# One step earlier in the input and one product form changed: image 1's load in layer 0, v's projection of images 6 and 7 in layer 1

## The chip, the cores and the metric

The kernel runs on one core of one Trainium2 chip. The metric is the device time of one execution in microseconds; 2955.44 us is the median of five executions before the change (2954.72 to 2956.1). Names of engines: PE is TensorE (matmuls), PEld its weight loads, DVE is VectorE, ACT is ScalarE, POOL is GpSimd, SP is the engine whose queue issues nearly all DMAs. All data are float32.

## What is computed

Eight images of 384 channels and 32 x 32 points pass through two attention layers. Cut to what matters here:

```python
# layer 0 (8 heads of 48): x = x + proj(softmax(q k^T * 48**-0.5 + relative_bias) v), qkv from group_norm(x)
# layer 1 (6 heads of 64): t = tokens of x
t = t + attn(layer_norm(t))     # q, k normalised per head, softmax, v, output projection
t = t + ffn(layer_norm(t))      # sign weights, groups of images 0..4 only; images 5..7 get zero
# v = layer_norm(t) @ qkv_w[v].T : for each image 1024 tokens x 384 channels -> 384
```

## The kernel before

**Units.** Both layers work image by image, and an image's attention is a list of units `(pair, h, m2)`: a pair of heads, one half of the queries, a quarter of the keys (32 units per image in layer 0, 24 in layer 1). `scores` makes two 128 x 1024 tiles of scores in PSUM (L746 in layer 0, L1722 in layer 1), DVE adds the relative bias in layer 0 (L757, two instructions per unit), ACT takes the exponent, and `weigh` of the unit two before multiplies with v (L777, L1771). PSUM has four such tiles for everything (`mm2`), SBUF nine tiles of 128 x 1024 for layer 0 (`etile`) and sixteen for layer 1 (`wtile`).

**Order.** The order of the instructions on each engine and queue is the order in which the program issues them. Side work is hung on a list, `later`: `later.after(n, work)` issues `work` at the n-th following step, and there is one step after each unit (`later.step()`), so a number there is a place in the order and not a time. An engine and the SP queue wait at each entry for what it needs, and everything issued after it on the same engine waits too.

**Layer 0, image 0.** While image 0's 32 units run, side work is done once for the whole kernel. The relative bias `grow` is loaded from a table in DRAM (`grow_load`, four DMAs of 114 KB into `oT`, L486) and turned round by ACT or DVE in turn (`grow_turn`, L496 and L498), one part per unit up to unit 16. The q and k weights are cut in two parts and a mixed part (`_cut_weights`, DVE, units 9 to 15 and 20 to 27) and stored to `cut`; v's weights are cut in the same way by `cut_weights_v` (L606 on: mask, subtract, mix, scale, three stores of 192 KB for each of three chunks) to `cut_v`, beginning at units 16, 17 and 18, the second halves two units later. Image 1's input `xn` is loaded at unit 12 (`load`, three DMAs of 512 KB, L343), and its group norm follows: `measure` (two statistics instructions per chunk, L513) at units 16, 17 and 18, a gather of two small DMAs, `scatter` (L527 on DVE, four POOL instructions, two DMAs) at unit 21, `apply` on ACT at units 24, 25 and 26. The masks for image 1's cut input follow at units 28, 29 and 31.

**One-pass products.** From image 1 on, layer 0 makes its projections as three products of cut operands: a high part (a mask clears the lowest 12 bits), a low part and a mixed part, each of type float32r. The profile has one matmul instruction and one weight load for each of these products, and two of each for a plain float32 matmul. `Ahead.project_v` (L698) makes layer 0's v so: 72 matmuls per image. Its stationary operand is `parts[..][:, ts(2 * m2 + i, P)]`, 128 neighbouring columns.

**Layer 1.** Images 0 to 4 have a feed-forward part, images 5 to 7 none. For images 6 and 7 `attention_inputs` makes q and k as one-pass products (`project_cut`, six blocks in the order 0, 1, 2, 4, 3, 5) from `Parts`, which holds the cut image, with weights that `_Cut.load` (L161, 576 KB each) brings into four slots (three in a tile `wc`, one in `more_cut`, shown as `wx`). Blocks 2 and 3 stay in their slots for good; blocks 0 and 1 are loaded at unit 3 of the image before, blocks 4 and 5 into the same slots when blocks 0 and 1 are done. Then `project_v` makes v as plain float32: 24 matmuls (48 instructions) per image, L1659. Its stationary operand takes every eighth column:

```python
xt[:, k].rearrange("c (p m) -> c m p", m=MT)[:, 2 * m2 + i],
wv[:, k], start=(k == 0), stop=(k == KC - 1),
```

DVE evicts it with a multiplication by the tokens' inverse deviation (L1669).

Of the kernel before, what the change touches and what calls it, by code (L numbers as in the profile page):

```python
# [19 lines left out]
F32 = mybir.dt.float32  # L20
F32R = mybir.dt.float32r
# [6 lines left out]
P = 128  # L28
# [27 lines left out]
NG = 5  # L56
# [43 lines left out]


BLOCKS = [(pair, s) for pair in range(KC) for s in range(2)]
BLOCKS1 = [(0, 1), (0, 0), (1, 1), (2, 1), (1, 0), (2, 0)]


# [94 lines left out]
class _Weights:  # L200
# [50 lines left out]
    def load_part(self, k, w):  # L251
        at = k * 3 * C
        self.nc.sync.dma_start(w, self.ready[:, at : at + 2 * C])

    def cut(self, k, w, tile):
        return _cut_weights(self.nc, k, w, tile, self.there)

# [14 lines left out]
        self.nc.sync.dma_start(self.image, self.x1[0].rearrange("(k p) n -> p k n", p=P))  # L272


def _layer0(tc, ins, x1, sums, shared, weights, beside):

# [6 lines left out]
    with ExitStack() as ctx:  # L285
# [306 lines left out]
                    )  # L592
            return qk

        BB = len(BLOCKS) // 2
        cut = dram.tile([len(BLOCKS), P, 3, KC, P], F32, tag="cut", name="cut", bufs=1)
        cut_v = dram.tile([P, 3, KC, C], F32, tag="cutv", name="cutv", bufs=1)

        def cut_tile(name):
            return etile(name)[:, 0 : 2 * C]  # L600

        def cut_weights_v(k):

            w = wv[:, k]
            t = etile(f"cv{k}")
            high, mixed = t[:, 0:C], t[:, HALF : HALF + C]  # L606

            def first():
                _masked(nc, high, w)
                nc.sync.dma_start(cut_v[:, 0, k], high)  # L610
                nc.vector.tensor_sub(w, w, high)

            def second():
                _mixed(nc, mixed, w, high)
                nc.sync.dma_start(cut_v[:, 2, k], mixed)
                nc.vector.tensor_scalar_mul(w, w, CUT)
                nc.sync.dma_start(cut_v[:, 1, k], w)

            first()
            later.after(2, second)  # L620

        class Ahead:

# [290 lines left out]
        for k in range(KC):  # L914
# [7 lines left out]
            )  # L922
            for at, stage in zip(((9, 11, 13, 15), (20, 21, 22, 23), (24, 25, 26, 27))[k], stages):
                later.after(at + 1, stage)
        for k in range(KC):
            later.after(17 + k, lambda k=k: cut_weights_v(k))
        for b in range(B):
            held = []
            for i, u in enumerate(units):
                done = held.pop(0) if len(held) == LAG else None  # L930
                held.append(
                    (u, scores(b, qk, u, lambda: weigh(b, *done) if done else None))
                )
                if i == (12 if b == 0 else 1) and b + 1 < B:
                    xn = load(b + 1)
                    for at, stage in zip(
                        (5, 6, 7, 10, 13, *((14, 15) if b == 0 else (13, 13))),
                        group_norm(b + 1, xn),
                    ):
                        later.after(at, stage)  # L940
                if i == 3 and b > 0:
                    project_out(b - 1, residuals(b - 1, etile), range(NF0))
                if b == B - 1:
                    for at, work in beside:
                        if at == i:
                            work()
                later.step()
                if i == 28 and b == 0:
                    cuts = _Cut(
                        nc, cut, BLOCKS,  # L950
                        shared.pool.tile([P, KC * 3 * C], F32R, tag="w", name="wc"),
                    )
                    for n in range(BB):
                        cuts.load(n)
                if b in (1, 2, 3) and i == 12:
                    t = cut_tile(f"cw{b}")
                    weights.load_part(b - 1, t)
                    for at, stage in enumerate(
                        weights.cut(
                            b - 1, t, lambda name, b=b, t=t: t if name == "cl" else cut_tile(f"{name}1{b}")  # L960
                        )
                    ):
                        later.after(4 + at, stage)
                masks, rounds = ((28, 29, 31), ()) if b == 0 else ((25, 26, 27), (28, 29, 30))
                if b + 1 < B:
                    if i == masks[0]:
                        ahead = Ahead(b + 1, xn)
                    if i in masks:
                        ahead.mask(masks.index(i))
                    if i in rounds:  # L970
                        ahead.round(rounds.index(i))
# [373 lines left out]
            )  # L1345


def _layer1(tc, ins, x1, out, shared, start, there, before=None, check=None):

# [1 line left out]
    with ExitStack() as ctx:  # L1353
# [300 lines left out]
        def project_v(b, xt, m2, c=None, copy=nc.vector.tensor_copy):  # L1654
# [9 lines left out]
            if c is None:  # L1664
                copy(v[:, 2 * m2 : 2 * m2 + 2], pv[:, :, 0:C])
            else:
                for i in range(2):
                    m = 2 * m2 + i
                    nc.vector.tensor_scalar_mul(v[:, m], pv[:, i, 0:C], c[:, 1, m : m + 1])  # L1669
            later.step()  # L1670

        def scale_v(c, m2):
# [382 lines left out]
        def attention_inputs(b, xt, rest=(), sums=None, parts=None):  # L2055
# [17 lines left out]
            for i, n in enumerate(range(len(BLOCKS)) if parts is None else (0, 1, 2, 4, 3, 5)):  # L2073
                if parts is None:
                    project_qk(b, *BLOCKS[n], xt, qk, sq)
                else:
                    project_cut(b, n, parts, qk, sq)
                    if i < 2:
                        cuts.load(n + 4)
                    if i == 0:  # L2080
                        rest_of_units()
                if i == 1:
                    token_stats(f"a{b}", tk)
                pair = i // 2
                if i % 2 == 0 and pair > 0:
                    head(pair - 1, *((5, 4) if pair > 1 else (3, 3) if parts is None else (2, 4)))
            if parts is None:
                rest_of_units()
            for m2 in range(MT // 2):
                project_v(b, xt, m2, tk)  # L2090
            head(NP1 - 1, 4, 4)
            return qk, kc

# [17 lines left out]
        later.after(26, store_w2)  # L2111
        later.after(1, rest_of_pools)
        qk, kc = attention_inputs(0, xt)
        behind = cuts = parts = None
        for b in range(B):


# [7 lines left out]
            for i, u in enumerate(units):  # L2125
# [7 lines left out]
                if i == 3:  # L2133
# [9 lines left out]
                    if more and b > 0:  # L2143
                        if cuts is None:
# [4 lines left out]
                            )  # L2149
                            cuts.load(2)  # L2150
                            cuts.load(3)
                        cuts.load(0)
                        cuts.load(1)
                        parts = Parts(b + 1, ahead)
                        for k, at in enumerate((8, 10, 12)):
                            later.after(at - i, lambda k=k, parts=parts: parts.cut_high(k))
# [140 lines left out]
def tile_conv_attn_hybrid(ctx: ExitStack, tc: tile.TileContext, ins, out):  # L2297
    dram = ctx.enter_context(tc.tile_pool(name="x1", bufs=1, space=DRAM))
    x1 = dram.tile([B, C, N], F32, tag="x1", name="x1")
    ready = dram.tile([P, KC * 3 * C], F32, tag="ready", name="ready")  # L2300
    there = dram.tile([len(BLOCKS), P, 3, KC, P], F32, tag="there", name="there1")
    state = ctx.enter_context(tc.tile_pool(name="state", bufs=1))
    flag = state.tile([P, 1], mybir.dt.int32, tag="flag", name="flag")
    sums = state.tile([P, B, NP0, 2 * N // P], F32, tag="sums", name="sums")
    with ExitStack() as main, tc.manual_schedule():
        shared = _Shared(tc, main)
        start = _Start(tc, ready, x1, shared)
        before = _layer0(
            tc, ins, x1, sums, shared, _Weights(tc, ins, ready, there, shared),
            [(5, start.load_weights), (6, start.load_image)],  # L2310
        )
        _layer1(
            tc, ins, x1, out, shared, start, there, before,
            lambda temp: _range_check(tc, sums, flag, lambda name: temp(name, (P, HALF))),
        )

# [1 line left out]
    with tc.If(out_of_range > 0):  # L2318
        _layer0_shifted(tc, ins, x1)
        with ExitStack() as again, tc.manual_schedule():  # L2320
# [1 line left out]
            start = _Start(tc, ready, x1, shared)  # L2322
            start.load_weights()
            start.load_image()
            _layer1(tc, ins, x1, out, shared, start, there)


# [42 lines left out]
```

## Time and profile before

| what | value |
|---|---|
| median of five executions | 2955.44 us |
| the profiled execution | 2955.57 us, of which 2953.7 us span |
| PE busy | 2920.0 us, 99% of the span |
| DVE, ACT, POOL busy | 67%, 51%, 17% |
| granted TensorE clock, mean | 0.998 |
| layer 0, image 0: from the first scores to the next image's projections | 75.41 to 202.04 us |
| layer 1, v of image 6 (L1659) | from 2660.33 to 2675.91 us |

The page's first part gives busy time, share of the span and instructions of each engine. In the timeline a row is: start in us, duration in us, engine, line, operation, output from input, shape, number of instructions, and in brackets the idle time before it and what ended it. In the table of stretches each engine has its busy time and its count, then the granted clock (1.00 is full speed), the share of the DMA engines, and GB/s.

### The profile page before, as it was taken

To read this page: it belongs to the slowest core of one execution; us is meant where nothing else is said; L and a number is where in the kernel's file an instruction comes from. 1 tells how busy PE (TensorE), PEld (TensorE's weight loads), DVE (VectorE), ACT (ScalarE), POOL (GpSimd) and SP (SyncE) were. 2 spreads that over 40 slices of the span, in tenths; PEclk is the share of its full clock that TensorE was granted. 3 is DMA by queue.
4 is the path that set the end of the run, shared out by engine and by line. 5 is a ranking of instruction groups with operands and counts; after the bars stand their busy time and mean duration, and the time that the engine had idled before them with its cause. 6 is when DMAs were issued, how large, how long until landed. Compare 5 with 4: busy or idle time off the path is not lost.

```text
span 2953.7 us, 47525 instructions
## 1 busy us (share of the span) xinstructions
PE 2920.0 (99%) x19538; PEld 1692.7 (57%) x19538; DVE 1970.3 (67%) x2005; ACT 1507.9 (51%) x1846; POOL 492.7 (17%) x312
## 2 busy tenths in 40 slices
PE   8999999999999999999999999999999999999998
PEld 3345565657565666644545647647647647655553
DVE  3786858676676757564655875875875875875756
ACT  2553626354453626353553555555555555564644
POOL 3020202121110202112202202302302302301020
PEclk9999999999999999999999999999999999999999
DMA  7643141312212140323311212112112112112111
GB/s 195 177 136 94 45 128 39 114 59 70 75 52 93 25 127 17 95 80 104 80 56 31 83 32 72 67 31 72 67 32 71 67 32 72 67 40 83 40 46 39
DMA packets 131971, 214.36 MB, mean 73 GB/s; under 512 B 62144, under 2 KB 81072, under 8 KB 130368
## 3 DMA queue, kind: packets, MB, share of 16 engines
q1 hardware_dynamic: 128480, 209.39, 24.0%
q8 instruction: 157, 2.57, 0.4%
q10 hardware_dynamic: 3264, 1.82, 0.2%
q14 instruction: 70, 0.57, 0.1%
HBM read 161.83 MB, written 40.28 MB: 68 GB/s over the span
## 4 chain that ended last, share of the span: by engine, by line
PE 92%; DVE 3%; DMA 2%; ACT 1%; issue 1%; SPq 0%; POOL 0%; DVEq 0%; ACTq 0%
PE s L746 15%; PE o L777 15%; PE s L1722 11%; PE o L1771 11%; PE pg L170 6%; PE y2p L2016 6%; PE y1p L1965 5%; PE pp L845 4%; PE pv L1659 4%; PE pm L170 3%; PE pp L1868 3%; PE vg L698 2%; PE pq L1511 2%; PE pq L572 1%; PE vm L698 1%; DVE qk L1592 1%
## 5 line engine op out<-in xcount | busy, mean ns | idle before, releaser
L761 ACT ACTIVATE e<-e 128x1024 f32<-128x1024 f32 x512 | 535.2, 1058 | 345.0 <-DVE e L757 328.7
L757 DVE TENSOR_TENSOR e<-s,grow 128x1024 f32<-128x1024 f32 x512 | 601.3, 1219 | 161.9 <-PE s L746 142.5
L746 PE MATMUL s<-qk 48*64 48x512 f32 x4096 | 613.6, 592 | 6.8 <-DVE e L757 6.8
L777 PE MATMUL o<-e,v 64*64 64x512 f32 x4096 | 608.4, 590 | 1.2 <-DVE e L757 1.2
L1733 ACT ACTIVATE e<-s,kc 128x512 f32<-128x512 f32 x768 | 464.6, 695 | 173.5 <-PE s L1722 164.0
L1722 PE MATMUL s<-qk,qk 64*64 64x512 f32 x3072 | 419.0, 592 | 2.8 <-DVE oT L1781 2.6
L1771 PE MATMUL o<-e,v 64*64 64x512 f32 x3072 | 414.5, 590 | 0.0
L746 PEld LDWEIGHTS s<-qk 48*64 48x64 f32 x4096 | 229.6, 132 | 247.7 <-issue 102.4
L777 PEld LDWEIGHTS o<-e,v 64*64 64x64 f32 x4096 | 250.1, 133 | 196.0 <-issue 104.8
L1722 PEld LDWEIGHTS s<-qk,qk 64*64 64x64 f32 x3072 | 153.5, 132 | 193.7 <-issue 109.0
L1748 DVE TENSOR_TENSOR t<-t,e 128x1024 f32<-128x1024 f32 x192 | 231.1, 1222 | 45.5 <-ACT e L1733 45.4
L1771 PEld LDWEIGHTS o<-e,v 64*64 64x64 f32 x3072 | 159.3, 133 | 169.5 <-issue 142.4
L806 POOL TENSOR_TENSOR inv<-sums,over 128x16 f32<-128x16 f32 x32 | 96.0, 2999 | 853.4 <-DMA sums<-sd 787.0
L1952 DVE TENSOR_REDUCE parts<-y 128x1 f32<-128x1024 f32 x75 | 89.7, 1217 | 103.3 <-ACT y L1949 102.9
L1745 DVE TENSOR_TENSOR t<-e,e 128x1024 f32<-128x1024 f32 x96 | 114.2, 1224 | 58.4 <-ACT e L1733 58.4
L1628 POOL TENSOR_TENSOR hc<-hc,rsqrt 128x32 f32<-128x32 f32 x24 | 137.6, 5735 | 2.0
L1659 PE MATMUL pv<-wv,bx 128*128 128x384 f32 x384 | 128.3, 491 | 0.0
L1868 PE MATMUL pp<-oT,L_attn_proj_wT 128*128 128x512 f32 x288 | 126.3, 595 | 1.6 <-DVE oT L1834 1.6
L845 PE MATMUL pp<-oT,wp 128*128 128x512 f32 x288 | 125.7, 595 | 0.0
L1659 PEld LDWEIGHTS pv<-wv,bx 128*128 128x128 f32 x384 | 119.4, 314 | 9.8 <-ACT e L1733 4.1
L673 DVE SCALAR_TENSOR_TENSOR qk<-pg,qk 128x1024 f32<-128x1024 f32 x42 | 51.5, 1225 | 100.0 <-PE pg L170 73.9
L1965 PE MATMUL y1p<-lun,w 128*128 128x512 f32 x360 | 113.4, 396 | 2.7 <-DVE lun L1915 2.7
(225 smaller groups left out, 3584.7 us busy)
## 6 DMA issues: line engine op xcount, KB each, us to landing
rb<-rd SPq DMA_DIRECT2D x110, 256.0 KB
wc<-there SPq DMA_DIRECT2D x25, 576.0 KB
wc<-cut SPq DMA_DIRECT2D x24, 576.0 KB
xn<-in_x_dram SPq DMA_DIRECT2D x24, 512.0 KB
res<-in_x_dram SPq DMA_DIRECT2D x24, 512.0 KB
x<-res SPq DMA_DIRECT2D x24, 512.0 KB
bx<-x SPq DMA_DIRECT2D x8, 1536.0 KB
rq<-hi SPq DMA_DIRECT2D x48, 256.0 KB
```

The source lines that it names most:

```text
L170: self.nc.tensor.matmul(out[:, h], w[:, i, k], part[k][:, ts(h, HALF)], start=(k == 0 and i != 1), stop=(k == KC - 1 and i != 0),)
L746: nc.tensor.matmul(s[j][ts(c, QP), i], qk[pair][rows, 1, ts(4 * m2 + 2 * i + c, QP)], qk[pair][rows, 0, ts(h, HALF)], start=True, stop=True,)
L757: nc.vector.tensor_add(e.rearrange("p (i q) -> p i q", i=2), s[j], bass.AP(near.tensor, near.offset, [near.ap[0], [-QROWS * IW, 2], [1, HA ...
L761: nc.scalar.activation(e, e, AF.Exp)
L777: nc.tensor.matmul(po[ts(j, S0), r], v[keys, 2 * m2 + i, 2 * pair + j, :], es[j][keys, ts(i, HALF)], start=(m2 == 0 and i == 0), stop=(m2 ...
L845: nc.tensor.matmul(pps[b, m][:, h], (wp[:, k] if k < NF0 else wl)[:, ts(m, P)], oT[:, k, ts(h, HALF)], start=(k == 0), stop=(k == (NF0 if ...
L1659: nc.tensor.matmul(pv[:, i, 0:C], xt[:, k].rearrange("c (p m) -> c m p", m=MT)[:, 2 * m2 + i], wv[:, k], start=(k == 0), stop=(k == KC - 1),)
L1722: nc.tensor.matmul(s[j][ts(c, QP), i], qk[pair, 1][rows, ts(4 * m2 + 2 * i + c, QP)], qk[pair, 0][rows, ts(h, HALF)], start=True, stop=True,)
L1733: nc.scalar.activation(e[:, ts(i, HALF)], s[j][:, i], AF.Exp, scale=kc[:, pair, j, m : m + 1])
L1748: nc.vector.tensor_add(total[j], total[j], e)
L1771: nc.tensor.matmul(po[ts(j, D1), r], v[keys, 2 * m2 + i, at : at + D1], es[j][keys, ts(i, HALF)], start=(m2 == 0 and i == 0), stop=(m2 == ...
L1965: nc.tensor.matmul(py[m][:, h], w1[:, k, ts(m, P)], un[k][i][:, ts(h, HALF)], start=(k == 0 and i == 0), stop=(k == KC - 1 and i == 1),)
```

## The change

In layer 0, image 0, the load of image 1 moves from unit 12 to unit 16, and the steps of its group norm move closer together: `measure` at units 18, 19 and 20, `scatter` at 22, `apply` at 24, 25 and 26 as before. `cut_weights_v` returns its two halves; they are issued at units 16 and 17, 18 and 20, 21 and 28 for the three chunks.

In layer 0, images 4 to 6, layer 1's weights of v are loaded a chunk at a time at unit 12 (192 KB), cut on DVE at units 16 and 18, and stored to a new DRAM tensor `there_v` (three stores of 192 KB).

In layer 1, at unit 3 of image 5, `load_weights_v` loads the three parts of v's weights (576, 576, 384 and 192 KB): the high part into the place of `wv`, the low part into `more_cut`, the mixed part into two of the sixteen `wtile`s, which stay taken to the end of image 7's projection. So the slots for blocks of q's and k's weights become three: block 2 is loaded again for image 7, and blocks 3, 4 and 5 are loaded after blocks 0, 1 and 2. `project_v_cut` replaces `project_v` for images 6 and 7: 72 one-pass matmuls instead of 48 instructions, two PSUM tiles instead of one per step, and an eviction by ACT and DVE for each m, with factors `cs` made by two POOL instructions.

```diff
-        def cut_weights_v(k):
-            w = wv[:, k]
-            t = etile(f"cv{k}")
-            high, mixed = t[:, 0:C], t[:, HALF : HALF + C]
+        def cut_weights_v(name, w, there, k):
+            tiles = []
             def first():
+                tiles.append(etile(name))
+                high = tiles[0][:, 0:C]
                 _masked(nc, high, w)
-                nc.sync.dma_start(cut_v[:, 0, k], high)
+                nc.sync.dma_start(there[:, 0, k], high)
                 nc.vector.tensor_sub(w, w, high)
             def second():
...
-            first()
-            later.after(2, second)
+            return first, second
...
-        for k in range(KC):
-            later.after(17 + k, lambda k=k: cut_weights_v(k))
+        for k, at in enumerate(((16, 17), (18, 20), (21, 28))):
+            for when, stage in zip(at, cut_weights_v(f"cv{k}", wv[:, k], cut_v, k)):
+                later.after(when + 1, stage)
...
-                if i == (12 if b == 0 else 1) and b + 1 < B:
+                if i == (16 if b == 0 else 1) and b + 1 < B:
                     xn = load(b + 1)
                     for at, stage in zip(
-                        (5, 6, 7, 10, 13, *((14, 15) if b == 0 else (13, 13))),
+                        (3, 4, 5, 7, 9, 10, 11) if b == 0 else (5, 6, 7, 10, 13, 13, 13),
                         group_norm(b + 1, xn),
...
+                if b in (4, 5, 6) and i == 12:
+                    t = cut_tile(f"cwv{b}")[:, 0:C]
+                    weights.load_part_v(b - 4, t)
+                    for at, stage in enumerate(cut_weights_v(f"cwx{b}", t, there_v, b - 4)):
+                        later.after(4 + 2 * at, stage)
...
+        def load_weights_v():
+            high = const.tile([P, KC, C], F32R, tag="wv", name="wvh")
+            low = more_cut.rearrange("p (k c) -> p k c", k=KC)
+            nc.sync.dma_start(high.bitcast(F32), there_v[:, 0])
+            nc.sync.dma_start(low.bitcast(F32), there_v[:, 1])
+            mixed = []
+            for at, n in ((0, 2), (2, 1)):
+                t = wtile(f"wvd{at}", (P, n, C), F32R)
+                nc.sync.dma_start(t.bitcast(F32), there_v[:, 2, at : at + n])
+                mixed.extend(t[:, k] for k in range(n))
+            return [high[:, k] for k in range(KC)], [low[:, k] for k in range(KC)], mixed
+
+        def project_v_cut(b, parts, m2, cs):
+            ps = [mm2(f"v{g}{b}_{m2}") for g in "gm"]
+            for i in range(2):
+                for part in (2, 0, 1):
+                    for k in range(KC):
+                        of = (parts.high, parts.low, parts.mixed)[part][k]
+                        nc.tensor.matmul(
+                            ps[part // 2][:, i, 0:C],
+                            of.rearrange("c (p m) -> c m p", m=MT)[:, 2 * m2 + i],
+                            weights_v[part][k],
+                            start=(k == 0 and part != 1), stop=(k == KC - 1 and part != 0),
+                        )
+            for i in range(2):
+                m = 2 * m2 + i
+                nc.scalar.activation(
+                    v[:, m], ps[1][:, i, 0:C], AF.Identity, scale=cs[:, 1, m : m + 1]
+                )
+                nc.vector.scalar_tensor_tensor(
+                    v[:, m], ps[0][:, i, 0:C], cs[:, 0, m : m + 1], v[:, m], ALU.mult, ALU.add
+                )
+            later.step()
...
-                    if i < 2:
-                        cuts.load(n + 4)
+                    if i < 3:
+                        cuts.load(n + 3)
...
+                    if parts is not None:
+                        cs = small.tile([P, 2, MT], F32, tag="cs", name=f"cs{b}")
+                        for n, by in enumerate((1.0 + 1.0 / CUT, -1.0 / CUT)):
+                            nc.gpsimd.tensor_scalar(
+                                cs[:, n], tk[:, 1], by, 1.0, ALU.mult, ALU.mult
+                            )
...
+                        if b == NG:
+                            cuts.slots = cuts.slots[: BB]
+                            weights_v = load_weights_v()
                         cuts.load(0)
                         cuts.load(1)
+                        if b > NG:
+                            cuts.load(2)
```

## The prediction

> **What bounds the kernel now.** The page's first part says who is busy: PE, nearly all the time. A gain must therefore shorten PE's own work or close one of its few gaps.
>
> ```profile
> PE 2920.0 (99%) x19538; PEld 1692.7 (57%) x19538; DVE 1970.3 (67%) x2005; ACT 1507.9 (51%) x1846; POOL 492.7 (17%) x312
> ```
>
> The waits of PE come next: the largest during attention is for DVE's bias addition, and the timelines of PE, DVE and SP put it into image 0, at unit 16.
>
> ```profile
> PE s L746 <- DVE e L757: 6.8, 4, 4.0
> ...
> 133.37 2.83 PE L746 MATMUL s<-qk 48*64 48x512 f32 x11 [4.00 <-DVE e L757]
> ...
> 131.53 0.65 DVE L498 COPY grow<-oT 128x480 f32<-128x480 f32 x1 [4.75 <-DMA oT<-table]
> ...
> 119.52 1.89 SPq L818 DMA_DIRECT2D rb<-rd  x2
> 121.84 1.32 SPq L343 DMA_DIRECT2D xn<-in_x_dram  x3
> 123.26 6.70 SPq L486 DMA_DIRECT2D oT<-table  x8
> ```
>
> DVE stands 4.75 us before a turn of the bias table, whose load was issued right behind image 1's three input DMAs. A table by stretches of image 0 shows what follows: the stalled unit, then a stretch in which DVE is busy 28.44 of 30.94 us.
>
> ```profile
> 75.41:128.35 52.94, 52.94 (x478) 22.33 (x481) 44.02 (x45) 36.31 (x40) 5.50 (x3) 1.00 0.69 200
> 128.35:138.56 10.21, 6.21 (x39) 1.69 (x35) 4.85 (x6) 2.75 (x4) 0.00 (x0) 0.70 0.78 202
> 138.56:169.50 30.94, 26.94 (x231) 8.80 (x227) 28.44 (x39) 15.55 (x16) 6.27 (x6) 0.99 0.29 90
> ```
>
> For layer 1, I compare the two forms of v: the stretches of image 6's plain v and of layer 0's one-pass v, and the instructions of their lines (minimum/median/maximum ns).
>
> ```profile
> 2660.33:2675.91 15.58, 15.58 (x49) 14.75 (x48) 6.92 (x9) 1.43 (x2) 5.63 (x2) 1.00 0.16 38
> 214.91:227.40 12.49, 12.49 (x73) 12.49 (x72) 8.20 (x14) 0.00 (x0) 2.40 (x1) 1.00 0.72 203
> ...
> L1659 PEld LDWEIGHTS pv<-wv,bx x384: 312/313/338, 1420.4 to 2824.5; 128*128 128x128 f32 x192
> L1659 PE MATMUL pv<-wv,bx x384: 486/486/720, 1420.8 to 2824.9; 128*128 128x384 f32 x192
> ...
> L698 PEld LDWEIGHTS vm<-wx,xd x168: 187/188/188, 214.7 to 1221.8; 128*128 128x128 f32 x168
> L698 PE MATMUL vm<-wx,xd x168: 334/334/342, 214.9 to 1222.0; 128*128 128x384 f32 x168
> ```
>
> The one-pass form of layer 0 takes 12.49 us for 72 matmuls, 173 ns each, against 15.5 for the plain one (48 at 323 ns). But layer 0 loads neighbouring columns (188 ns a load); layer 1 takes every eighth column, and its loads last 313 ns. Under 323 ns of streaming that is hidden; under 173 it would not be. How much of a load counts is read where PE comes out of other work: the first load and matmul of a stage.
>
> ```profile
> 2660.10 0.88 PEld L1659 LDWEIGHTS pv<-wv,bx 128*128 128x128 f32 x3
> ...
> 2660.33 0.82 PE L1659 MATMUL pv<-wv,bx 128*128 128x384 f32 x2
> ...
> 1965.74 1.36 PE L1659 MATMUL pv<-wv,bx 128*128 128x384 f32 x3
> ```
>
> **The sum's base.** The profiled execution took 2955.57 us, 2953.7 of it span; it lies 0.13 above the median of 2955.44. The sum is made against 2955.57 and then lowered by 0.13.
>
> **Image 0, the load at unit 16: -6.8 us.** Units follow each other every 3.44 us; unit 16 took 10.21, so 6.77 were lost: 4.00 idle, the rest at a granted clock of 0.70 over that stretch. The three input DMAs are 1536 KB; at the 290 GB/s of the stretch 126 to 133 us they take 5.4 us, and 1.3 us of SP's issue time. Without them the table's part has only `rb` (512 KB) ahead of it and comes some 6 us earlier, more than the 4.75 that DVE waited. At unit 16 the input is behind the last table load (132.21) and the store of the q weights (134.94) and ahead of v's stores and the sums of pair 1, whose user is POOL, with no PE work waiting. It then has two units (6.9 us) to land before its statistics, for 5.4 us of bytes of which the first third suffices. Bounds: -4 (another transfer still late) to -7.
>
> **Image 0, DVE's work spread: -1.6 us.** A unit leaves DVE 3.44 - 2.36 = 1.08 us beside its two additions. By the timeline's durations (turn 0.65, statistics of a chunk 1.28, first half of v's cut 0.91, second half 0.91, q/k cut 0.55 or 0.95, aggregate 0.78, oT's addition 0.69) the extras of units 16 to 22 were 2.84, 2.88, 3.10, 0.91, 1.46, 2.42, 0.95: 14.6 us against an allowance of 7.6, so 7.0 too much; PE lost 30.94 - 7 x 3.44 = 6.9 there, of which one wait of 1.78 before the addition at 162.33 has no releaser named and falls where v's tiles wait for their stores in the queue. After: 1.56, 1.60, 2.19, 1.28, 2.74, 2.55, 1.73, together 13.65: only 0.9 less, since just one half moves out (to unit 28). The gain lies between 0.6 (0.9, less 0.3 at units 28 and 29, where 1.6 and 1.38 meet 1.08) and 2.4 (the 1.78 too); I take the middle. So DVE stays late by some 5 us here.
>
> **Closer steps of the group norm: 0.** The gather has two units instead of three: from its first DMA (151.31) to its second (153.82) and as long again is 5 us, under 6.9. From `scatter` to `apply` on ACT: aggregate at 164.93, last DMA issued 168.67, landing some 2 us on: 5.8 us under 6.9. With that cover gone ACT waits, and its exponents behind it: up to 1 us.
>
> **Layer 0, images 4 to 6: +0.4.** 1.8 us of DVE over two units, each 0.91 under the allowance of 1.08, and four DMAs of 192 KB. Nearest row: images 1 to 3 cut q and k's weights (3.0 us of DVE) and are 166.1 us apart at the start of their projections, the later ones 165.85; so 0.25 for 3.0, and 0.15 here. Bounds 0 to 0.75.
>
> **Layer 1, the loads at unit 3 of image 5: 0.** 1728 KB on SP behind image 6's input (issued 2559.2) and ahead of blocks 0 and 1; these are used at 2627.9, 60 us later. SP's next entry is at 2605.
>
> **v in one pass: +2.15 us an image, +4.3.** Old: 48 x 0.323 = 15.5. New: 72 matmuls, each behind a load of every eighth column. The bounds of their spacing: 173 ns if the load hides as in layer 0, 313 ns if a whole load lies between two matmuls. The rows above decide between them. At 1965.74 the load had no cover: three matmuls took 1.36 instead of 2 x 0.323 + 0.486 = 1.13, and the longest one 720 instead of 486: 0.23 us exposed. At 2660.10 the load began with a one-pass matmul; the next matmul came 0.23 us later, and it and its successor took 0.82 instead of 0.81. So 0.23 to 0.25 from load to streaming, and a load starts with the matmul before: spacing 0.245, 72 x 0.245 = 17.65. Cover of the rest: eviction adds eight ACT instructions per image (nearest: oT's copy, 0.59 us each, 4.7 us in all) where ACT is busy 1.43 of 15.6 us, DVE's stay eight (0.56 for 0.61); PSUM's two tiles per step are read during the next step's 4.4 us. The two POOL instructions (0.3 each) fall where POOL idles before 2653.
>
> [...]
>
> **Three weight slots: +0.2.** Block 4 is now loaded behind block 1, not block 0: its place in SP's queue is that at 2645.45 (behind `rb`), the packets there end at 2650.24, and block 4's matmuls begin at 2650.53. Block 5 waits for block 2's matmuls (2650.9) and is used at 2656.0; such a load issued at 2632.38 ended at 2636.86. Each covers by 0.3 to 0.7 us; all of PE is queued behind. Behind block 5's DMA on SP stands pair 0's chain of norms (`hd`, `hc`, `hi`, `rq`), some 3 us later now; its user on DVE is issued after v's third step, at about 2673.5, and `rq` would land by 2669. Bounds 0 to 2.
>
> **Two tiles fewer of sixteen in layer 1: +0.4.** Units 13 to 17 hold six exponents, two totals, four folded sums and two or three of the next image's: 14 or 15. So for a few units an exponent waits for `weigh` of the unit before the last, about 0.5 us, on ACT, which has 1 us per unit spare. Bounds 0 to 5 (0.5 us in five units of two images).
>
> **Sum.** -6.8 - 1.6 + 0.4 + 4.3 + 0.2 + 0.4 = -3.1: 2952.5 from the profiled execution, 2952.4 against the median. That is 0.1%, less than the 0.2% (5.9 us) that a measurement of this kernel can tell from no change.
>
> **The rivals.**
> - Loads hide: spacing 0.173, v 12.5, -3.0 an image instead of +2.15. Sum -3.1 - 10.3 = -13.4: 2942. For it, layer 0's stage; against it, the 0.23 us between load and matmul in three places. 9%.
> - Slower: a whole load of 313 ns between matmuls: 22.5 us, +7 an image, sum -3.1 - 4.3 + 14 = +6.6: 2962. Beyond a spacing of 0.267 us ((15.5 + 3.7)/72) the kernel is slower than before, beyond 0.307 by 0.2%. For it, the loads' own durations; against it, matmuls that start before a load's record ends. 10%.
> - Image 0's stall doesn't go: a later part of the table, the statistics or `apply` takes its place, and 2 of 8.4 us are won: 2959. For it, SP's queue is in order and DVE is overfull to unit 22; against it, the bytes above. 9%.
> - Fourteen tiles bind for eight units an image, 0.5 to 1 us each: +8 to +16, 2960 to 2968. 6%.
> - The likeliest, as summed, 66%, its own range 2949.5 to 2956.
>
> **Range and chances.** 2947 to 2960.5 leaves out the first rival, most of the second and part of the fourth: about 2 in 10. Faster by over 0.2% (under 2949.5): the first rival and a tenth of the likeliest, 16%. Slower by over 0.2% (over 2961.4): two thirds of the second, half of the fourth, a little of the rest, 12%. Within: 72%.
>
> **What would show it.** Right: no wait of DVE for `oT<-table` near 131 us and full clock there; DVE still nearly full in units 17 to 23 with PE losing 4 to 6 us; v of images 6 and 7 17 to 18 us long with PEld busy throughout. Wrong: v at 12.5 or 22 us, a wait of a load at block 4, or waits before exponents in units 13 to 17 of images 5 and 6.

## The result: slightly slower, and the profile after

The changed kernel takes 2957.97 us (median of 24 executions) against 2955.39 us (44 executions of the kernel before, on the same chips): a ratio of 1.001, with a 95% interval of 1.0004 to 1.0015. The forecast of 2952.4 us had the wrong sign. The change is small, but effects of 4 to 16 us lie in it with different signs; that 2957.97 still lies within the stated range of 2947 to 2960.5 is luck, because terms that the sum did not have stand against each other. The profiled execution took 2962.07 us, of which 2960.3 us span; it lies 4.1 us above its median, while that of before (2955.57 us) lies 0.2 above its own. So the stages are compared between the two profiles, and the totals between medians.

The page's first part for the changed kernel gives the busy time of each engine:

```profile
PE 2920.6 (99%) x19586; PEld 1700.4 (57%) x19586; DVE 1976.6 (67%) x2017; ACT 1516.1 (51%) x1862; POOL 488.8 (17%) x316
```

PE's busy time is the same as before to 0.6 us. The answer is therefore not in the sums, but in the gaps. PE's waits after:

```profile
PE pm L171 <- DMA wc<-there: 11.7, 3, 5.6
PE ph L450 <- DMA w<-in_L_conv_mlp_w_dram: 8.0, 2, 7.6
PE s L750 <- DVE e L761: 3.9, 4, 1.5
PE pp L1913 <- DVE oT L1879: 3.7, 4, 1.4
```

The wait for DVE in layer 0's attention has gone from 6.8 to 3.9 us. At the top stands a wait that the table of before did not have: the projections of q and k in layer 1 (`pm`, L171) wait for a load of weights (`wc`). The table of stretches gives the stages that the prediction spoke of (us; busy time and count of PE, PEld, DVE, ACT, POOL; granted clock, DMA share, GB/s): image 0 up to unit 16, unit 16 and what follows it, then a block of image 6's projection and image 6's v.

```profile
75.37:128.32 52.95, 52.95 (x478) 22.29 (x481) 45.24 (x47) 36.30 (x40) 5.51 (x3) 1.00 0.65 185
128.32:138.63 10.31, 10.31 (x100) 3.90 (x96) 9.63 (x14) 7.08 (x8) 0.00 (x0) 1.00 0.91 290
138.63:169.50 30.87, 28.43 (x256) 10.32 (x252) 29.64 (x37) 18.35 (x20) 6.57 (x6) 1.00 0.39 111
2639.74:2646.14 6.40, 6.40 (x18) 5.08 (x19) 0.00 (x0) 1.02 (x1) 4.79 (x2) 0.63 0.03 8
2655.73:2673.14 17.41, 17.41 (x74) 17.23 (x73) 6.91 (x9) 5.68 (x10) 5.63 (x2) 1.00 0.14 33
```

In the second row, 10.31 us hold 100 matmuls at full clock, where they held 39 before: three units instead of one. In the last row v takes 17.41 us for its 72 one-pass matmuls, with PEld busy throughout. The fourth row is block 4 of image 6's q and k: 18 records in 6.40 us at a granted clock of 0.63.

Set side by side, the start of each stage on PE (first matmul, before and after) tells where the time goes. Negative is earlier after the change:

| stage | before, us | after, us | difference | change since the row above |
|---|---|---|---|---|
| projections after layer 0's image 0 | 201.97 | 194.55 | -7.42 | -7.42 |
| attention of image 5, layer 1 | 2542.32 | 2530.37 | -11.95 | -4.53 |
| q and k of image 6 | 2627.88 | 2615.65 | -12.23 | -0.28 |
| v of image 6 | 2660.33 | 2655.73 | -4.60 | +7.63 |
| attention of image 6 | 2676.91 | 2674.13 | -2.78 | +1.82 |
| q and k of image 7 | 2777.26 | 2775.24 | -2.02 | +0.76 |
| v of image 7 | 2809.70 | 2815.77 | +6.07 | +8.09 |
| attention of image 7 | 2826.28 | 2834.17 | +7.89 | +1.82 |

So: 7.4 us won in image 0; 4.5 us won after it, in images whose code the diff barely touches; 15.7 us lost before v, in the projections of q and k; 3.6 us lost in v itself.

The loss before v is one wait per image. PE's timeline at block 4 of image 6, and its first row in image 7:

```profile
2639.74 2.04 PE L171 MATMUL pm<-pw,wc 128*128 128x512 f32 x4 [5.44 <-DMA wc<-there]
2641.59 1.05 PE L171 MATMUL pm<-xd,wc 128*128 128x512 f32 x2
2642.44 3.86 PE L171 MATMUL pg<-pw,wc 128*128 128x512 f32 x12
2646.14 1.09 PE L171 MATMUL pm<-pw,wc 128*128 128x512 f32 x4
...
2799.46 2.04 PE L171 MATMUL pm<-pw,wc 128*128 128x512 f32 x4 [5.57 <-DMA wc<-there]
```

SP's queue just ahead of it:

```profile
2632.03 1.15 SPq L1870 DMA_DIRECT2D rb<-rd  x2
2633.22 1.05 SPq L162 DMA_DIRECT2D wc<-there  x2
```

PE was ready for block 4 at 2639.74 - 5.44 = 2634.30, only 1.1 us after the load had been issued behind `rb`. With it went block 5's load (x2): from 2633.22 to 2639.74 the DMA engines moved 259 GB/s, 1.69 MB, nearly what `rb` (512 KB) and both transfers of 576 KB hold together, and block 4's weights came 6.5 us after their issue. Then the gap costs a second time. The granted clock after it, from the table of stretches:

```profile
2639.74:2642.44 2.70, 2.70 (x6) 2.12 (x7) 0.00 (x0) 0.00 (x0) 1.09 (x2) 0.50 0.07 18
2642.44:2644.00 1.56, 1.56 (x5) 1.27 (x4) 0.00 (x0) 1.02 (x1) 1.56 (x1) 0.50 0.00 0
2644.00:2646.14 2.14, 2.14 (x9) 1.69 (x9) 0.00 (x0) 0.00 (x0) 2.14 (x1) 0.90 0.00 0
2646.14:2648.00 1.86, 1.86 (x9) 1.50 (x8) 1.23 (x1) 0.33 (x1) 0.86 (x1) 1.00 0.05 8
```

The clock is 0.50 for more than 4.2 us; block 4 takes 6.40 us, where the same block before took 4.30 (2646.46 to 2650.76). The wait and the slow block, 5.44 + 2.10, make 7.5 of the 7.63 us.

Theory after this reading: block 4's late load cost some 15.7 us in two images, the distance of v's columns some 5 us each, and without both the changed kernel would beat the one before. Rivals: the loss belongs to the changed order of work in general (three slots, fourteen tiles) and would not go with the load; v's matmuls are slow for another reason than their columns; and the 4.5 us in the middle are noise between two executions, or come from something that the change does unnoticed.

### The profile page after: what moved, and what is told of

Its sections match the earlier page's. It is cut to its first block, busy times and chain, and to the rows that moved or that the text cites. A ratio compares the mean times of both kernels' runs of the same rounds, so it can differ in the third digit from the quotient of the medians.

```text
span 2960.3 us, 47672 instructions
## 1 busy us (share of the span) xinstructions
PE 2920.6 (99%) x19586; PEld 1700.4 (57%) x19586; DVE 1976.6 (67%) x2017; ACT 1516.1 (51%) x1862; POOL 488.8 (17%) x316
## 3 DMA queue, kind: packets, MB, share of 16 engines
q10 hardware_dynamic: 3264, 1.82, 0.2%
## 4 chain that ended last, share of the span: by engine, by line
PE 90%; DVE 4%; DMA 2%; ACT 2%; issue 1%; SPq 0%; POOL 0%; DVEq 0%; ACTq 0%
PE s L750 15%; PE o L781 14%; PE s L1767 11%; PE o L1816 10%; PE pg L171 6%; PE y2p L2061 6%; PE y1p L2010 5%; PE pp L849 4%; PE pm L171 3%; PE pv L1669 3%; PE pp L1913 3%; PE vg L702 2%; PE pq L1521 2%; PE pq L577 1%; DMA rb<-rd 1%
## 5 line engine op out<-in xcount | busy, mean ns | idle before, releaser
L1602 DVE SCALAR_TENSOR_TENSOR qk<-pg,qsq 128x1024 f32<-128x1024 f32 x36 | 57.7, 1603 | 97.0 <-PE pg L171 68.3
L2010 PE MATMUL y1p<-un,w 128*128 128x512 f32 x360 | 112.7, 394 | 0.3 <-ACT qsq L1537 0.3
```

The costliest lines, as they stand in the source:

```text
L2010: nc.tensor.matmul(py[m][:, h], w1[:, k, ts(m, P)], un[k][i][:, ts(h, HALF)], start=(k == 0 and i == 0), stop=(k == KC - 1 and i == 1),)
```

## The experiments

Each result is the median of 4 to 11 executions (given as n) beside the kernel before on the same chip. That kernel's median varied between 2957.1 and 2959.3 us there, so ratios are compared, or starts of stages; each kernel has one profiled execution.

**The two halves alone.** `img0` is the kernel before with the edits in layer 0's image 0; `v_only` is the changed kernel without them.

```diff
 # v_only, against the changed kernel
-                if i == (16 if b == 0 else 1) and b + 1 < B:
+                if i == (12 if b == 0 else 1) and b + 1 < B:
...
-        for k, at in enumerate(((16, 17), (18, 20), (21, 28))):
-            for when, stage in zip(at, cut_weights_v(f"cv{k}", wv[:, k], cut_v, k)):
-                later.after(when + 1, stage)
+        for k in range(KC):
+            later.after(17 + k, lambda k=k: cut_v_as_before(k))
```

> The edit of image 0 alone (input at unit 16, v's cut spread), layer 1 as before. Theory A (image 0 gives about 7.4 us, and the changed kernel loses them in layer 1 at block 4's weights): 2948 us, the projections after image 0 begin at 194.6 instead of 202.0 us. Theory B (image 0's gain is given back later in layer 0 or in the feed-forward images): 2953 to 2956. One-pass matmuls of 512 columns in the feed-forward part (y1p, y2p) stay 0.232 us apart if their pace of 0.227 in the changed kernel has to do with the edit of layer 1; 0.227 if it has to do with image 0's edit.

> The edit of layer 1 alone (with the cuts in layer 0's images 4 to 6), image 0 as before. Theory A: slower by some 10 us (2965): block 4's wait of 5.5 us plus 2 us of slowed clock in each of two images, v 17.4 us instead of 15.6 in each, less some 4 us if the feed-forward matmuls go at 0.227. Theory C (block 4's wait is an accident of the shifted times): the wait of the matmuls for the block's load is absent or under 1 us and the time is 2958 to 2960.

Measured: `img0` 2949.04 us (n = 6), ratio 0.9968 (0.9956 to 0.9981); `v_only` 2969.14 us (n = 5), ratio 1.0035 (1.0022 to 1.0049), both against 2957.44. Image 0's edits gain 8.4 us, layer 1's lose 11.7; together that is +3.3, where the changed kernel measured +2.6. In `img0` the projections after image 0 start at 194.87 us, 7.1 earlier than before. In `v_only`'s trace image 0 alone was 3.0 us slower than in that of before, with the same code there: its waits for DVE were 7.8 and 2.6 us. From the first scores to the next image's projections, the five traces with image 0 as before (`before`, `v_only`, `pad`, `pad64`, `pad256`) take 126.6 to 129.5 us, the six with both edits 119.0 to 119.2. The trace of before is the shortest of its five, which can explain why the medians give image 0 more than the 7.1 to 7.4 us of the traces.

**Block 4's load one step earlier.** In the changed kernel `project_cut` ends with a step of `later`, and that step issues the pair's `rd` and `rb` on SP ahead of the load. `early` issues the load first, for blocks 3, 4 and 5 alike, and changes nothing else.

```diff
-                    project_cut(b, n, parts, qk, sq)
+                    project_cut(b, n, parts, qk, sq, step=False)()
                     if i < 3:
                         cuts.load(n + 3)
+                    later.step()
```

> The changed kernel, with the loads of blocks 3 to 5 issued ahead of the step instead of behind it, so block 4's load stands before the inverse sums and rb in SP's queue. Theory A: block 4's load is issued at the end of block 1 (4.3 us before block 4's matmuls instead of 1 us) and the wait shrinks to under 1 us in each image; total 2946 to 2949. Rival D (the transfer itself is the limit, because two weight blocks and rb share the DMA engines): a wait of 3 us or more stays and the time is above 2952.

Measured: 2946.0 us (n = 5), ratio 0.996 (0.9946 to 0.9973). SP's and PE's timelines of `early`:

```profile
2630.11 0.32 SPq L162 DMA_DIRECT2D wc<-there  x1
2631.60 0.32 SPq L1863 DMA_DIRECT2D rd<-inv  x1
2633.88 1.15 SPq L1870 DMA_DIRECT2D rb<-rd  x2
2635.12 0.53 SPq L162 DMA_DIRECT2D wc<-there  x1
```

```profile
2634.21 1.06 PE L1617 MATMUL hs<-qsq,heads 128*32 128x512 f32 x8
2635.20 1.20 PE L171 MATMUL pm<-pw,wc 128*128 128x512 f32 x4
2636.24 0.63 PE L171 MATMUL pm<-xd,wc 128*128 128x512 f32 x2
```

Block 4's load now stands ahead of `rd` and `rb`, alone, 5.1 us before its use, and the matmuls follow without a wait. From `after` to `early` the stretch from q and k to v shrinks by 7.60 us in image 6 and 8.05 in image 7: 15.65 us, the whole loss. The order of the loads against `rd` and `rb` decided the sign of the change. Three slots and fourteen tiles are still there, so they do not by themselves cause this loss. The edit also parts block 4's load from block 5's (2635.12), so how much of the delay was the place behind `rb`, and how much the bytes of block 5, is not told apart.

**Neighbouring columns for v.** `neigh` is `early` with the stationary operand of v taken as in layer 0.

```diff
-                            of.rearrange("c (p m) -> c m p", m=MT)[:, 2 * m2 + i],
+                            of[:, ts(2 * m2 + i, P)],
```

> The kernel with the early loads, and v's stationary operand for images 6 and 7 made of 128 neighbouring columns instead of every eighth: the rows of v come in another order, so attention in these two images weighs the wrong tokens; the amount of work is the same. Theory (the distance of the columns in the weight load sets v's pace): loads of 188 ns, 72 matmuls 0.173 us apart, v 12.5 us instead of 17.4, the kernel 2 x 4.9 = 10 us faster than with the early loads (2934). Rival (the pace comes from the three operands' places or from two PSUM tiles per step): spacing stays 0.242 and the time 2944 to 2946.

Measured: 2937.28 us (n = 4), ratio 0.9921 (0.9906 to 0.9936). The lines of v in the changed kernel, and then in `neigh` (duration in ns: minimum, median, maximum):

```profile
L1701 PEld LDWEIGHTS vg<-wvh,pw x48: 337/338/342, 2656.2 to 2831.9; 128*128 128x128 f32 x48
L1701 PE MATMUL vg<-wvh,pw x48: 401/403/410, 2656.4 to 2832.1; 128*128 128x384 f32 x48
```

```profile
L1701 PEld LDWEIGHTS vg<-wvh,pw x48: 187/188/188, 2649.6 to 2808.1; 128*128 128x128 f32 x48
L1701 PE MATMUL vg<-wvh,pw x48: 334/334/343, 2649.8 to 2808.2; 128*128 128x384 f32 x48
```

With the columns side by side a load lasts 188 ns instead of 338, and v is shorter by 4.80 us in both images: from 17.40 to 12.60 us. Nothing else was changed but the order of v's rows (so the attention of these images weighs the wrong tokens, with the same amount of work): the distance of the columns costs 0.07 us per matmul, and without it one-pass v gains 3 us per image on the plain form. The distance here is 32 bytes; no run tries another.

**Why the middle is faster: a tile that nobody reads.** Between image 0 and image 6 the diff does almost nothing on PE, but it adds the small tile `cs` to layer 1 (two buffers of 64 bytes per partition). By the order of the program, all that is placed behind it moves by 128 bytes, among it the weights of the feed-forward. `pad` is the kernel before with such a tile and one write to it; `pad64` and `pad256` move the rest by 64 and 256 bytes.

```diff
+        pad = small.tile([P, 2, MT], F32, tag="cs", name="cs0")   # pad; pad64: [P, 8]; pad256: [P, 32]
+        nc.gpsimd.memset(pad, 0.0)
```

> The kernel before, with one small tile (128 x 16 floats) more in layer 1's pool of small tiles, written once and never read, so that the tiles behind it lie 64 or 128 bytes further on in SBUF. If the place of the feed-forward's operands sets the pace of their matmuls, y1p and y2p go from 0.232 to 0.227 us and the time falls by some 4 us (2951). If the pace differs from execution to execution, both stay as they were: 2955.4.

> The kernel before with an unread tile of 128 x 8 floats, so the feed-forward weights lie 64 bytes further on instead of 128. If any shift away from the place in the kernel before will do, y1p and y2p are 0.227 us apart or less and the time is 5 to 6 us under the kernel before; if the place counts in steps of 128 bytes, they stay at 0.232 and the time does not change.

> The kernel before with an unread tile of 128 x 32 floats: a shift of 256 bytes. If the pace depends on the place within 256 bytes, this is as in the kernel before: 0.232 us and no gain. If the place within a larger unit counts, 0.227 or another value.

Measured: `pad` 2951.64 us (n = 11), ratio 0.998 (0.9971 to 0.9989); `pad64` 2953.41 (n = 10), 0.9988 (0.9978 to 0.9998); `pad256` 2956.68 (n = 10), 1.0001 (0.9991 to 1.001). The groups of instructions (busy us, mean ns of one) show which matmuls are quicker. For before, the second product of the feed-forward:

```profile
L2016 PE MATMUL y2p<-hy,w 128*128 128x512 f32 x360 | 114.6, 399 | 0.0
```

For the changed kernel, `pad`, `pad64` and `pad256`, in that order:

```profile
L2061 PE MATMUL y2p<-hy,w 128*128 128x512 f32 x360 | 112.5, 394 | 0.0
```

```profile
L2018 PE MATMUL y2p<-hy,w 128*128 128x512 f32 x360 | 112.5, 394 | 0.0
```

```profile
L2018 PE MATMUL y2p<-hy,w 128*128 128x512 f32 x360 | 113.3, 396 | 0.0
```

```profile
L2018 PE MATMUL y2p<-hy,w 128*128 128x512 f32 x360 | 114.6, 399 | 0.0
```

From one start to the next, the median is 0.232 us in the kernel before, 0.227 with the 128 bytes (in `pad` as in the changed kernel), and 0.232 again with 256, in both products of the feed-forward. With 64 bytes it is 0.229 in the second product, and in the first 0.228 with one moving operand (`un`) and 0.235 with the other (`lun`), although both meet the same weights. There are 1440 such matmuls in the five images, so 5 ns make at most 7.2 us. Counted from the end of image 0 to the attention of image 5, `pad` gains 3.1 us on the kernel before in the two traces, the changed kernel 4.5, and `img0_pad` (below) 6.5 on `img0`; single executions differ by some 2.5 us in this stretch. Over all traces the two groups do not meet: 2340.4 to 2342.9 us in the six kernels without the 128 bytes, 2334.5 to 2337.2 in the seven with them. An unread tile is thus enough for a gain like the -4.53 of the table: it belongs to a shift by 128 bytes. Why the place matters is not shown. By the order of the pools in the program (the traces show no addresses) the weights move and, with them, the moving operand `un` (pool `wide`), while `lun` and the second product's operands `hy` and `ly` stay; all four go from 0.232 to 0.227. So the distance between weights and moving operand does not account for it, as it is unchanged for `un`; nor do the weights alone, as they have two paces in `pad64`.

**Image 0's two edits apart, and with the shift.** `img0_load` has the load at unit 16 and the closer group norm, `img0_cut` the spread halves of v's cut, each in the kernel before; `img0_pad` is `img0` with `pad`'s tile.

```diff
 # img0_load: the first two; img0_cut: the third
-                if i == (12 if b == 0 else 1) and b + 1 < B:
+                if i == (16 if b == 0 else 1) and b + 1 < B:
...
-                        (5, 6, 7, 10, 13, *((14, 15) if b == 0 else (13, 13))),
+                        (3, 4, 5, 7, 9, 10, 11) if b == 0 else (5, 6, 7, 10, 13, 13, 13),
...
+        for k, at in enumerate(((16, 17), (18, 20), (21, 28))):
```

> Only the load of image 1 at unit 16 and its closer group norm, v's cut in image 0 as before. By the prediction's terms the load is worth 6.8 us and the spread 1.6 of the 8.4 that the edit of image 0 gave: 2948 to 2949, against 2947 with both. Rival (the stall's gain is only won together with the spread, because DVE is too full at units 16 to 18): under 4 us, 2952.

> Only v's cut in image 0 spread to units 16 to 28, the load of image 1 still at unit 12. The stall at unit 16 stays; the spread gives 0.6 to 2 us: 2953 to 2955 (against 2955.4). The marks of load alone and of both lie 1.2 us apart, so 1.2 if the two parts are separate.

> Image 0's edit together with the unread tile of 128 x 16 floats, layer 1 otherwise as before. If the two effects are separate and add up: -8.4 and -5.8 us, 2941 (against 2955.4). If the tile's gain was one of timing that image 0's edit brings as well: 2946 to 2949.

Measured: `img0_load` 2949.13 us (n = 5), ratio 0.9964 (0.9951 to 0.9978); `img0_cut` 2954.46 (n = 10), 0.9989 (0.998 to 0.9999); `img0_pad` 2940.21 (n = 5), 0.9938 (0.9924 to 0.9952). From the first scores to the projections after image 0, the load alone gains 6.2 us on the trace of before, and load and cut 7.4, so the cut gives 1.2 on top. By itself it gives nothing at that place, where the late load still stalls the units (PE's waits for DVE there are 8.8 us). Whether `img0_cut`'s 2.7 us in the median are its own stays open: its trace takes 126.6 us for image 0, as before, and ends only 0.6 us earlier. The shift and image 0's edits simply add: 0.9968 x 0.998 = 0.9948, against 0.9938 with an interval that holds it.

**A version that keeps v's order.** `turned` writes the cut parts of images 6 and 7 in the order in which v reads them, so that v's columns are neighbours; q is turned back as it is written, k needs no turning.

```diff
 # on top of early and neigh, for images 6 and 7
-                nc.vector.tensor_copy(self.high[k], t)
+                nc.vector.tensor_copy(
+                    self.high[k].rearrange("c (m p) -> c m p", m=MT),
+                    t.rearrange("c (p m) -> c m p", m=MT),
+                )
...
 # project_cut, where s == 0; k's part and the low part are left out here
+                        to = t.rearrange("c (p m) -> c m p", m=MT)
+                        of, with_ = (x.rearrange(by_m, m=MT) for x in (flat2(ps[0]), q))
```

> As the kernel with the early loads, but the cut parts of images 6 and 7 are written in the order of v's rows when they are cut (DVE writes or reads at a distance of eight for the high and the low part, q is turned back when it is taken, k no longer has to be). v's loads then take neighbouring columns and all results are in place. v 12.5 us; if DVE's longer instructions stay in units' spare time, 2934 to 2937; if they delay the units (up to 2 us in each of units 16 to 18 in two images) 2938 to 2946.

Measured: 2938.14 us (n = 5), ratio 0.993 (0.9917 to 0.9944): 21 us below the kernel before, and level with `neigh`, which leaves v's rows in another order. But `img0_pad`, without any of layer 1's edits, stands at 2940.21 beside it, and the two intervals overlap. Against `img0_pad`, v is 3.0 us shorter in each image, but the units ahead of the two projections are 3.2 and 2.0 us longer (one execution each). Of that, one part is in every kernel with one-pass v. ACT's timeline of the changed kernel, in the units of images 5 and 6:

```profile
2585.53 3.59 ACT L1778 ACTIVATE e<-s,kc 128x512 f32<-128x512 f32 x6 [2.46 <-DVE f L1798]
...
2745.06 3.58 ACT L1778 ACTIVATE e<-s,kc 128x512 f32<-128x512 f32 x6 [2.46 <-DVE f L1798]
```

An exponent stands 2.46 us until DVE has folded a sum (`f`), where the change from one pair to the next leaves the fewest tiles; the kernel before and `img0_pad` have no such wait. From the first scores of an image to those of its last unit but one, PE takes 75.5 us in image 5 and 91.2 in image 6 in the eight kernels with plain v, and 76.9 and 92.6 in the five with one-pass v, within 0.1 each: 1.4 us in each image. That the two tiles taken are the cause is read from what ends the wait; no run gives them back. A second part may be the turning. DVE's timeline in `turned` and then in `img0_pad`, at the same work on image 7's input:

```profile
2741.44 2.01 DVE L1583 TENSOR_TENSOR pw<-bx,pw 128x1024 fp32r<-128x1024 f32 x1
```

```profile
2741.10 1.22 DVE L1568 TENSOR_TENSOR pw<-bx,pw 128x1024 fp32r<-128x1024 f32 x1
```

A subtraction that reads one operand at a distance of 32 bytes takes 2.01 us instead of 1.22, three times per image. DVE is busy 40.5 of 43.9 us there (38.7 of 43.4 in `img0_pad`), and PE waits for DVE at the last unit:

```profile
2610.64 2.04 PE L1794 MATMUL s<-qk,qk 64*64 64x512 f32 x16 [1.80 <-DVE oT L1853]
```

From the last unit but one to the last it is 5.4 and 5.3 us in `turned`, 1.4 and 1.0 more than in `early`. But the same step takes 5.4 us in image 5 of the kernel before and 5.2 in image 6 of `v_only`, which turn nothing, so these 2.4 us are not shown to come from the turning. One-pass v thus gains 6.0 us in the two images and loses 2.8 in the units ahead; the rest is not settled, and 2 us of difference in the medians are not told apart from nothing. Another place than two `wtile`s for v's mixed part was not tried.

## Why the prediction was wrong

**Step "Three weight slots: +0.2": the step that failed.** It predicted the right place (block 4's load takes the place behind `rb` at 2645.45, its packets end at 2650.24), but gave block 4's first matmul as 2650.53. The trace of before, PE and SP:

```profile
2646.46 1.20 PE L170 MATMUL pm<-pw,wc 128*128 128x512 f32 x4
...
2650.76 1.09 PE L170 MATMUL pm<-pw,wx 128*128 128x512 f32 x4
```

```profile
2644.26 1.14 SPq L1825 DMA_DIRECT2D rb<-rd  x2
2645.45 0.58 SPq L161 DMA_DIRECT2D wc<-there  x1
```

The blocks run in the order 0, 1, 2, 4, 3, 5. The matmuls from 2650.5 on read `wx`, and that slot holds block 3; block 4's are those at 2646.46, 1.0 us after the load's place in the queue. (2650.53 is the first weight load of block 3.) The same slip of one place puts block 2's end at 2650.9; it is at 2645.5, so block 5's load could follow block 4's at once, as it did. Read rightly, the same rows would have given a wait of 2650.24 - 2646.46 = 3.8 us in each image, plus the clock: image 0's 4.00 us of idle time, in the same trace, cost 6.77 with the slow clock behind it. As a rough estimate in that proportion, 3.8 makes 6.4 us, and the sum would have been -3.1 - 0.2 + 2 x 6.4 = +9.5, with the sign right. Measured were 7.63 and 8.09: block 4's matmuls began 6.5 us after the load's issue, where the row of before has 4.8 from issue to the last packet. The bounds given, 0 to 2, were drawn around a cover that did not exist. A late slot was not among the rivals, though the last paragraph named a wait of a load at block 4 as what would show the prediction wrong; it did.

**The term that was missing: -4.5.** No step spoke of the place of tiles in SBUF. `cs` moved the feed-forward's weights (and `un`) by 128 bytes and made 1440 matmuls 5 ns quicker. The trace of before has nothing that would show it.

**The clock after the wait.** The stretches above put it at 0.50 for more than 4.2 us, then at 1.00. In finer stretches it is 0.50 from 2637.60 to 2644.42, 6.8 us, of which the first 2.1 fall into the wait and 4.7 on matmuls; in image 7 5.4 us fall on matmuls (2799.46 to 2804.86), and behind image 0's wait in the kernel before 5.9 (133.37 to 139.27). The 0.63 and 0.70 of longer stretches are mixtures of 0.50 and 1.00. What sets the length of the stretch at 0.50 is not shown.

**Image 0: right.** Predicted -6.8 for the load and -1.6 for the spread cut, measured -6.2 and -1.2 between the traces, -8.4 for both in the median. DVE stayed full, as forecast: 29.64 of 30.87 us in the third stretch above. PE is idle 2.4 us in it and waits 3.9 for DVE in the whole image, somewhat less than the 4 to 6 us named.

**v in one pass: right.** The spacing was forecast as 0.245 us, and is 17.41 / 72 = 0.242; the rows of exposed loads carried further than the 173 and 313 ns at the ends. The stage grew by 1.82 us an image instead of 2.15. The rival "loads hide" would need neighbouring columns: `neigh`, with them, takes 12.6 us.

**Two tiles fewer, "+0.4": a wait in the right place, but taken too small.** The step let an exponent wait 0.5 us for `weigh` in a few units, which ACT would absorb. It is one wait in each image, 2.46 us long, for a folded sum, and PE loses 1.4 us by it: 2.8 in all, inside the bounds of 0 to 5. The rival of eight late units did not come.

**Layer 0's cuts in images 4 to 6: right, nearly nothing.** Between image 0's end and the end of layer 0 the difference between the two traces moves by 0.05 us, where 0.4 was expected.

**The sum.** With the measured stages it is -7.4 - 4.5 - 0.3 + 7.6 + 1.8 + 0.8 + 8.1 + 1.8 = +7.9 at the start of image 7's attention; 1.3 are given back to the end (+6.6 of span). The medians say +2.6, the profiled execution of the changed kernel lying 4.1 above its own. `early`, without the wait, gives what the working would have without its misread row and with the missing term: -3.1 - 4.5 + 2.4 for the tiles makes -5.2. Between the two profiles it is -7.6, between the medians -11.4; the rest of 2 to 6 us is not accounted for, beside a spread of 5 us among the executions of `early`.

## What to carry to other kernels

When a buffer's reload is moved to another slot, name the instruction that reads the slot from its operand (here `wx` against `wc`) and not from its position in the list; then compare its start with the load's place in the queue, and price a late landing by what it cost here: the wait, and behind it a granted clock of 0.50 for 4.7 to 5.9 us of matmuls (three waits of 4.0 to 5.6 us). Ask of every entry ahead of such a load on the same queue what it waits for: issuing the loads before the step that holds `rd` and `rb` was worth 15.7 us without touching any work. And before a gain of 0.2% is put down to an edit, move the memory layout alone: an unread tile gave as much here.

## What the runs showed of the hardware that was not expected

- The pace of one-pass matmuls of 128 x 512 changed with the place of their operands in SBUF: one start every 0.232 us at the original place (`before`), 0.228 to 0.235 with the weights 64 bytes further on (`pad64`, by the moving operand), 0.227 at +128 (`pad`), 0.232 at +256 (`pad256`). In time: 2951.64 us against 2957.44 for a tile that nobody reads (two buffers of 64 bytes).
- A weight load of 128 columns of one-pass float32 took 188 ns with neighbouring columns (`neigh`) and 338 ns at a distance of 32 bytes (the changed kernel); one-pass matmuls of 384 columns started every 0.173 and 0.242 us.
- A DVE subtraction over 128 x 1024 that reads one operand at a distance of 32 bytes took 2.01 us (`turned`), with neighbouring elements 1.22 (`img0_pad`).
- Two loads of 576 KB in the same place behind `rb` landed at different times: in the changed kernel, with block 5's load issued right behind, block 4's matmuls began 6.5 us after the issue (259 GB/s in that time); in the kernel before, with no other load behind it, the packets ended after 4.8 us (233 GB/s). No run changes only what stands behind.
